# Layer 1's projection on raw rows: the mean in the matrix, 1/std in the eviction, results loaded three groups ahead

## The chip, the cores and the metric

The kernel runs on one core of a Trainium2 chip. The metric is device time in microseconds (us) of one execution; lower is better. Engines in this text: PE is TensorE (PEld its weight loads), DVE is VectorE, ACT is ScalarE, POOL is GpSimd, SP is SyncE, whose queue issues most transfers.

## The reference, cut to what matters

Two layers, each a graph attention and then a feed-forward part, on x of 3327 rows by 256. The part that the change touches is the entry of layer 1's attention:

```python
def _layernorm(x, axis=-1, eps=1e-5):
    m = jnp.mean(x, axis=axis, keepdims=True)
    v = jnp.var(x, axis=axis, keepdims=True)
    return (x - m) / jnp.sqrt(v + eps)

def _L1_gnn_ref(h, adj, W, a):
    wh = h @ W
    wh1 = wh @ a[:F_OUT, :]
    wh2 = wh @ a[F_OUT:, :]
    e = wh1 + wh2.T
    e = jnp.where(e > 0, e, ALPHA * e)
    e = jnp.where(adj > 0, e, NEG_BIG)
    attention = jax.nn.softmax(e, axis=-1)
    h_prime = attention @ wh
    return jax.nn.elu(h_prime)

x = x + _L0_gnn_ref(_layernorm(x), adj, ...)
x = x + _L0_ffn_ref(_layernorm(x)[None], ...)[0]      # 16 experts, the best 2 of each row
x = x + _L1_gnn_ref(_layernorm(x), adj, L1_gnn_W, L1_gnn_a)
x = x + _L1_ffn_ref(_layernorm(x)[None], ...)[0]      # 30 recurrent steps
```

So wh is the product of the normalized rows with W; the two score columns wh1 and wh2 are computed here as two more columns of the same product, from W a, so that the matrix has 258 columns.

## The kernel before, in words

x lies in SBUF as 26 tiles of 128 rows by 256. The stages follow each other: layer 0's projection, its attention, the experts (61 tiles of 128 listed rows, about 397 to 746 us), layer 1's projection (752 to 811 us), layer 1's attention, and 30 recurrent steps (on PE from about 1113 us).

**The experts.** `work_off` (L784) runs one tile of rows at a time: two products with w1 and w2 (L773), silu and multiply (L801, L805), the product with w3 (L812), a scaling (L815), and a scatter of the rows to `given` in DRAM (L816). On the way, at tile 16, it loads layer 1's parameters (`layer1_parameters`, L322: the matrix gW into `wv1`, the vectors ga, and `ones_r`, a tile of ones), and at tile 22 `score_vectors` (L334) computes the two score columns of `wv1`.

**Layer 1's projection.** `groups1` (L45) cuts the 26 tiles into seven groups: group 0 has two tiles, groups 1 to 6 have four. For each group:

- `add_results` (L885) loads the two results of every row from `given` (L891, two transfers on SP's queue into the buffers `th` and `z`, which have two copies each), adds them (L892, on POOL; for group 0 on DVE), and adds the sum to x (L894, DVE). Groups 0 and 1 are asked for ahead of the loop, group g + 2 while group g is worked on.
- `normalized` (L108) takes mean and variance on DVE (L114, L115), variance plus epsilon (`ve`, L117), its power -1/2 on POOL (`rstd`, L119), minus mean times rstd on POOL (`low`, L122, L123), and writes the normalized rows `xn` on ACT (L125, scale and bias of each row).
- `turned` (L133) transposes two tiles of `xn` on PE (L139, four instructions into a PSUM bank) and copies them to `hT` on ACT (L140).
- `products` (L149) multiplies each of the two tiles with `wv1` (L153, two matmuls of 258 columns a tile, each of them two records in the trace), one pair of tiles behind the transposes.
- `split1` (L904) evicts a product: 256 columns to `wh` on ACT (L905), the two scores to `sc.s` on DVE (L906). At a group's end `Scores.finish` (L180) makes exponentials on ACT (L181 to L183, full, part and row) and `minus` on DVE (L184).

The products go to six PSUM places (three names, two copies), the transposes to two. After the stage, `attend` (L188) transposes the row factors (L208, copied in L212), makes edges on ACT (L239), masks them on DVE (L244) and multiplies on PE (L249).

**What sets the order.** Each engine has one queue of instructions, in which it works in order. The tile framework's scheduler places the instructions of the stages into these queues; so on DVE the statistics of one group stand between the additions and the scores of others, and on POOL the order of the additions and of `rstd` and `low` is fixed: rstd, low and low of group 0, additions 1 and 2, rstd, low and low of group 1, addition 3, and so on. `project` and `normalized` serve layer 0 too, where normalized rows are written on DVE (L128).

Of the kernel before, what the change touches and what calls it, by code (L numbers as in the profile page):

```python
# [3 lines left out]

# [6 lines left out]
F32 = mybir.dt.float32  # L11
# [3 lines left out]
AF = mybir.ActivationFunctionType  # L15
ALU = mybir.AluOpType
# [3 lines left out]
P = 128  # L20
# [4 lines left out]
G = 4  # L25
MOST = 6
# [3 lines left out]
def gat_moe_gat_recurrent_ffn(ctx: ExitStack, tc: tile.TileContext, a: dict, out: bass.AP):  # L30
    nc = tc.nc
    N, D = a["x"].shape
    KD = D // P
# [9 lines left out]
    groups = [range(t, min(t + G, NT)) for t in range(0, NT, G)]  # L43
# [23 lines left out]
    x = state.tile([P, NT, D], F32, name="x")  # L67
# [37 lines left out]
    )  # L105
    nc.vector.tensor_scalar(real, real, 0.0, None, op0=ALU.is_gt)

    def normalized(src, dst, scale=1.0, by_act=False):  # L108

        n = len(src)  # L110
        mv = small.tile([P, MOST, 2], F32, name="mv")
        for j in range(n):
            st = small.tile([P, 6], F32, name="st")
            nc.vector.bn_stats(st, src[j])  # L114
            nc.vector.bn_aggr(mv[:, j, :], st)  # L115
        ve = small.tile([P, MOST], F32, name="ve")
        nc.vector.tensor_scalar(ve[:, :n], mv[:, :n, 1], EPS, 1.0 / scale**2, op0=ALU.add, op1=ALU.mult)  # L117
        r = small.tile([P, MOST], F32, name="rstd")
        power = nc.gpsimd.tensor_tensor(r[:, :n], ve[:, :n], neg_half[:, :n], ALU.pow)  # L119
        if by_act:  # L120
            low = small.tile([P, MOST], F32, name="low")
            nc.gpsimd.tensor_tensor(low[:, :n], mv[:, :n, 0], r[:, :n], ALU.mult)  # L122
            nc.gpsimd.tensor_scalar(low[:, :n], low[:, :n], -1.0, None, op0=ALU.mult)  # L123
            for j in range(n):
                nc.scalar.activation(dst[j], src[j], AF.Identity, scale=r[:, j : j + 1], bias=low[:, j : j + 1])  # L125
            return power.ins
        for j in range(n):
            nc.vector.tensor_scalar(  # L128
                dst[j], src[j], mv[:, j, 0:1], r[:, j : j + 1], op0=ALU.subtract, op1=ALU.mult
            )  # L130
        return power.ins

    def turned(two, work, ps):  # L133

        pt = ps.tile([P, 2, KD, P], F32, name="bank")
        hT = work.tile([P, 2, KD, P], F32, name="hT")
        for j in range(2):
            for k in range(KD):
                nc.tensor.transpose(pt[:, j, k, :], two[:, j, k * P : (k + 1) * P], ident)  # L139
        nc.scalar.copy(hT, pt)  # L140
        return hT

    def project(groups, wv, n_out, finish, work, ps, ps_p, by_act, aside):

        pending = None

        def products(hT, t):  # L149
            for j in range(2):  # L150
                p = ps_p()
                for k in range(KD):
                    nc.tensor.matmul(  # L153
                        p[:, :n_out], lhsT=hT[:, j, k, :], rhs=wv[:, k, :], start=(k == 0), stop=(k == KD - 1)
                    )
                finish(t + j, p)

        for ts in groups:
            n = len(ts)
            xn = work.tile([P, G, D], F32, name="xn")  # L160
            power = normalized([x[:, t, :] for t in ts], [xn[:, j, :] for j in range(n)], 1.0, by_act)
            aside(ts, power)
            for j0 in range(0, n, 2):
                hT = turned(xn[:, j0 : j0 + 2, :], work, ps)
                if pending:
                    products(*pending)
                pending = hT, ts[j0]
        products(*pending)

    class Scores:  # L170
# [9 lines left out]
        def finish(self, t0, t1):  # L180
            nc.scalar.activation(self.full[:, t0:t1], self.s[:, t0:t1, 1], AF.Exp)  # L181
            nc.scalar.activation(self.part[:, t0:t1], self.s[:, t0:t1, 1], AF.Exp, scale=ALPHA)
            nc.scalar.activation(self.row[:, t0:t1], self.s[:, t0:t1, 0], AF.Exp, scale=1.0 - ALPHA)  # L183
            nc.vector.tensor_scalar(self.minus[:, t0:t1], self.part[:, t0:t1], -1.0, None, op0=ALU.mult)  # L184
# [149 lines left out]
    def score_vectors():  # L334

        for k in range(KD):
            for s in range(2):
                tc.keep_in_program_order(
                    nc.vector.scalar_tensor_tensor(
                        prod, wv1[:, k, :D], 1.0, va[:, s, :], op0=ALU.mult, op1=ALU.mult,  # L340
                        accum_out=wv1[:, k, D + s : D + s + 1],
                    )
                )

    with ExitStack() as moe:
# [25 lines left out]
        def bank():  # L371
            return ps.tile([P, 512], F32, name="bank")

        with ExitStack() as pre:
# [63 lines left out]
                if ts is groups[3]:  # L438
                    take_graph(groups0[0], behind)

            project(groups, wv, D + 2 * H, split0, work, ps, bank, False, first_rows)
            nc.vector.tensor_scalar(wh[:, NT - 1], wh[:, NT - 1], real[:, 0:1], None, op0=ALU.mult)
            for ts in groups0[1:3]:
                behind = take_graph(ts, behind)
# [339 lines left out]
        def work_off(s0, s1, aside):  # L784

            hT = features_first(ahead.popleft())
            made = None
            for s in range(s0, s1 + 1):
                if s == FIRST:
                    for _ in aside:  # L790
                        pass
                    layer1_parameters()
                if s == FIRST + 6:
                    score_vectors()
                hidT = made
                if s < s1:
                    if s + 4 < s1:
                        ahead.append(gathered(s + 4))
                    pa = product(hT, ew[s % SETS][0])
                    act = edge("e")  # L800
                    nc.scalar.activation(act, pa, AF.Silu)  # L801
                    next(aside, None)
                    pb = product(hT, ew[s % SETS][1])
                    made = edge("pT")
                    nc.vector.tensor_tensor(made, act, pb, ALU.mult)  # L805
                    if s + 1 < s1:
                        hT = features_first(ahead.popleft())
                if s > s0:
                    w3 = ew[(s - 1) % SETS][2]
                    po = ps_o.tile([P, 512], F32, name="acc1")[:, :D]  # L810
                    for f in range(FH):
                        nc.tensor.matmul(po, lhsT=hidT[:, f, :], rhs=w3[:, f, :], start=(f == 0), stop=(f == FH - 1))  # L812
                    y0 = 6 * KD * HID + s % 2 * D
                    y = sets[1][:, y0 : y0 + D]
                    nc.vector.tensor_scalar(y, po, weight[:, s - 1 : s], None, op0=ALU.mult)  # L815
                    put = nc.gpsimd.indirect_dma_start(  # L816
                        out=given, out_offset=bass.IndirectOffsetOnAxis(ap=to[:, s - 1 : s], axis=0), in_=y,
                        in_offset=None,
                    )
                    tc.declare_no_dep(put.ins, group="given", reason="no two results have the same row")  # L820
                    tc.add_to_no_dep_group("given", put.ins)
                if s + SETS - 1 < s1:
                    weights(s + SETS - 1)
                next(aside, None)
# [52 lines left out]
    with ExitStack() as st:  # L877
# [4 lines left out]
        work = st.enter_context(tc.tile_pool(name="work2", bufs=2))  # L882
        ps = st.enter_context(tc.tile_pool(name="ps2", bufs=2, space=PSUM))
        ps_o = st.enter_context(tc.tile_pool(name="ps2o", bufs=2, space=PSUM))
        def add_results(some):  # L885
            for ts in some:
                n, two = len(ts), []
                for k, name in enumerate(("th", "z")):
                    here = slice(k * NP + ts[0] * P, k * NP + (ts[-1] + 1) * P)
                    two.append(steps.tile([P, G, D], F32, name=name)[:, :n, :])  # L890
                    nc.sync.dma_start(two[k], given[here, :].rearrange("(t p) d -> p t d", p=P))  # L891
                (nc.vector if ts is groups1[0] else nc.gpsimd).tensor_tensor(two[0], two[0], two[1], ALU.add)  # L892
                here = x[:, ts[0] : ts[-1] + 1, :]
                nc.vector.tensor_tensor(here, here, two[0], ALU.add)  # L894

        add_results(groups1[:2])
        count = 0

        def spot():
# [1 line left out]
            count += 1  # L901
            return ps_o.tile([P, 512], F32, name=f"acc{count % 3}")

        def split1(t, p):  # L904
            nc.scalar.copy(wh[:, t, 0, :D], p[:, :D])  # L905
            nc.vector.tensor_copy(sc.s[:, t, :, 0], p[:, D : D + 2])  # L906
            for ts in groups1:
                if t == ts[-1]:
                    sc.finish(ts[0], t + 1)

        project(
            groups1, wv1, D + 2, split1, work, ps, spot, True,
            lambda ts, power: add_results(groups1[groups1.index(ts) + 2 :][:1]),
        )
        nc.vector.tensor_scalar(wh[:, NT - 1], wh[:, NT - 1], real[:, 0:1], None, op0=ALU.mult)

# [144 lines left out]
```

## Time and profile before

| what | us |
|---|---|
| runs: median (lowest to highest of 3) | 2020.62 (2019.47 to 2022.0) |
| the profiled execution | 2019.73 |
| its span | 2017.6 |
| PE, DVE, ACT, POOL busy over the span | 1937.5, 1300.5, 1106.0, 955.3 |
| last scatter of the experts issued | 746.39 |
| first result transfer of layer 1 issued | 752.52 |
| first transpose of layer 1's projection | 760.97 |
| last product of the projection ends | 808.1 |
| first product of layer 1's attention | 811.25 |

The profile is of one execution. In its tables an entry such as "x4" counts instructions; a timeline line has the start in us from the span's start, the busy time, the engine, the line of the code, the operation with output<-inputs, and in brackets how long the engine idled before and what ended the idling. A line of the waits has the waiting instruction, the one waited for, and the sum, the number and the longest of these waits in us. PEclk is the share of its full clock that PE was granted.

### The profile page before, as it was taken

The numbers are of one execution on the slowest core, as the hardware profiler recorded it, in microseconds if no ns is written. First come the engines' busy times: TensorE is split into PE (matmuls) and PEld (weight loads), VectorE is DVE, ScalarE is ACT, GpSimd is POOL, SyncE is SP. The second block draws the span as 40 slices with busy tenths as digits, with TensorE's granted clock in tenths as the row PEclk, the third lists the DMA queues.
The fourth block names the chain that finished last, engine by engine and source line by source line (L and its number), as shares of the span: only waits on it lengthen the run. The fifth ranks groups of instructions, "written<-read, shape, count | busy, mean of one in ns | idle before, by whom it ended". The sixth has DMA issues, their size and how long they took to land.

```text
span 2017.6 us, 33598 instructions
## 1 busy us (share of the span) xinstructions
PE 1937.5 (96%) x12028; PEld 1752.4 (87%) x12028; DVE 1300.5 (64%) x3845; ACT 1106.0 (55%) x1445; POOL 955.3 (47%) x884
## 2 busy tenths in 40 slices
PE   7999999999999977999999999999999999999998
PEld 6999999999999975888888888888888888888887
DVE  6887888732222215567676777777777777777777
ACT  2976766621111116666555665665666666666664
POOL 3020212453333315001000677877877887777785
PEclk9999999999999997999999999999999999999999
DMA  8978141199999853000000000000000000000003
GB/s 163 118 99 118 9 76 49 42 314 332 349 331 306 293 168 120 9 9 16 9 9 16 27 1 1 1 1 1 1 1 1 1 1 1 1 1 1 1 1 115
DMA packets 139754, 157.08 MB, mean 78 GB/s; under 512 B 52027, under 2 KB 99364, under 8 KB 139586
## 3 DMA queue, kind: packets, MB, share of 16 engines
q1 hardware_dynamic: 123466, 122.05, 19.8%
q0 software_dynamic: 11440, 28.09, 8.1%
q10 hardware_dynamic: 4680, 4.76, 0.7%
q8 instruction: 98, 1.61, 0.3%
q14 instruction: 70, 0.57, 0.1%
HBM read 164.58 MB, written 29.78 MB: 96 GB/s over the span
## 4 chain that ended last, share of the span: by engine, by line
PE 67%; issue 10%; POOL 5%; ACT 5%; DVE 4%; DMA 4%; SPq 0%; POOLq 0%; DVEq 0%; ACTq 0%
PE po L996 35%; PE acc L249 23%; PE pt L990 5%; ACT zT L992 5%; POOL given L816 2%; DVE pT L244 2%; POOL rb L717 2%; DMA given<-wh,to 2%; DMA wh<-in_w_dram 1%; DMA lists<-pair,ati 1%; PE acc L153 1%; PE bank L139 1%; PE bank L486 1%; POOL rstd L119 1%; PE bank L208 0%
## 5 line engine op out<-in xcount | busy, mean ns | idle before, releaser
L996 PE MATMUL po<-wc,zT 128*128 128x256 f32 x3120 | 706.1, 383 | 21.7 <-ACT zT L992 21.1
L996 PEld LDWEIGHTS po<-wc,zT 128*128 128x128 f32 x3120 | 583.5, 190 | 124.6 <-ACT zT L992 50.0
L249 PE MATMUL acc<-wh,pT 128*128 128x129 f32 (+1 forms) x4056 | 606.5, 311 | 2.0 <-DVE pT L244 1.8
L249 PEld LDWEIGHTS acc<-wh,pT 128*128 128x128 f32 x4056 | 561.7, 191 | 40.1 <-DVE pT L244 3.7
L239 ACT ACTIVATE e<-rb,minus,full 128x384 f32<-128x384 f32 (+3 forms) x494 | 400.4, 824 | 180.0 <-DVE pT L244 164.0
L982 POOL TENSOR_TENSOR th<-th,x 128x1024 f32<-128x1024 f32 (+1 forms) x210 | 459.9, 2206 | 64.0 <-ACT th L980 64.0
L244 DVE SCALAR_TENSOR_TENSOR pT<-e,part,adjT 128x384 f32<-128x384 f32 (+3 forms) x494 | 380.7, 774 | 138.4 <-PE acc L249 118.8
L1001 DVE SCALAR_TENSOR_TENSOR x<-po,rr,bb 128x256 f32<-128x256 f32 x780 | 324.8, 477 | 119.1 <-PE po L996 114.2
L992 ACT COPY zT<-pt 128x1024 f32<-128x1024 f32 (+1 forms) x210 | 199.1, 948 | 333.8 <-PE pt L990 333.8
L988 DVE BATCH_NORM_STATS2 stats<-z 128x6 f32<-128x256 f32 x780 | 283.6, 415 | 117.2 <-ACT z L983 117.2
L119 POOL TENSOR_TENSOR rstd<-ve,neg_half 128x4 f32<-128x4 f32 (+3 forms) x28 | 31.1, 1110 | 413.2 <-DVE ve L117 317.5
L971 POOL TENSOR_TENSOR rr<-rr,neg_half 128x4 f32<-128x4 f32 (+1 forms) x210 | 207.5, 988 | 17.4
L983 ACT ACTIVATE z<-th 128x1024 f32<-128x1024 f32 (+1 forms) x210 | 210.6, 1003 | 0.4 <-POOL th L982 0.3
L980 ACT ACTIVATE th<-x 128x1024 f32<-128x1024 f32 (+1 forms) x210 | 199.3, 995 | 2.2 <-DVE x L128 1.3
L990 PE MATMUL pt<-ident,z 128*128 128x128 f32 x1560 | 190.9, 273 | 2.5 <-DVE high L926 2.5
L990 PEld LDWEIGHTS pt<-ident,z 128*128 128x128 f32 x1560 | 178.6, 141 | 14.8 <-issue 2.9
L773 PEld LDWEIGHTS bank<-hT,wh 128*128 128x128 f32 x1280 | 149.2, 192 | 6.0 <-issue 1.7
L773 PE MATMUL bank<-hT,wh 128*128 128x128 f32 x1280 | 150.5, 275 | 3.2 <-DMA wh<-in_w_dram 3.2
L805 DVE TENSOR_TENSOR pT<-e,bank 128x512 f32<-128x512 f32 x61 | 41.9, 687 | 167.2 <-PE bank L773 167.1
L801 ACT ACTIVATE e<-bank 128x512 f32<-128x512 f32 x61 | 36.4, 597 | 195.2 <-PE bank L773 186.8
L816 POOL DMA_INDIRECT given<-wh,to x61 | 60.2, 987 | 165.7 <-DVE wh L815 148.4
L552 POOL DMA_INDIRECT lists<-pair,ati x52 | 61.1, 1176 | 133.9 <-DVE ati L539 43.5
(183 smaller groups left out, 1261.3 us busy)
## 6 DMA issues: line engine op xcount, KB each, us to landing
wh<-in_w_dram SPq DMA_DIRECT2D x120, 512.0 KB
first_set<-in_w_dram SPq DMA_DIRECT2D x63, 512.0 KB
in_bytes<-in_adj_dram POOLq DMA_DIRECT2D x3, 2496.0 KB, 28.3
x<-in_x_dram SPq DMA_DIRECT2D x6, 512.0 KB
th<-given SPq DMA_DIRECT2D x6, 512.0 KB
z<-given SPq DMA_DIRECT2D x6, 512.0 KB
kept<-x SPq DMA_DIRECT2D x8, 384.0 KB
old<-kept SPq DMA_DIRECT2D x6, 512.0 KB
```

The source lines that it names most:

```text
L239: nc.scalar.activation(e[:, : n * P], rb[:, : n * P], AF.Relu, scale=sc.full[:, j, h : h + 1], bias=sc.minus[:, j, h : h + 1],)
L244: masked = nc.vector.scalar_tensor_tensor(pT[:, : n * P], e[:, : n * P], sc.part[:, j, h : h + 1], adjT[:, j // 2, ts[0] * P : (ts[-1] + 1 ...
L249: nc.tensor.matmul(po[c], lhsT=pT[:, c * P : (c + 1) * P], rhs=wh[:, j, h, :], start=(j == 0 and c % per_bank == 0), stop=(j == NT - 1), s ...
L773: nc.tensor.matmul(p[:, f, :], lhsT=w[:, k, f * P : (f + 1) * P], rhs=hT[:, k, :], start=(k == 0), stop=(k == KD - 1),)
L971: nc.gpsimd.tensor_tensor(r[:, :n], r[:, :n], neg_half[:, :n], ALU.pow)
L982: nc.gpsimd.tensor_tensor(th[:, :n, :], th[:, :n, :], hs, ALU.add)
L983: nc.scalar.activation(z[:, :n, :], th[:, :n, :], AF.Silu, scale=1.0 / S)
L988: nc.vector.bn_stats(stats[:, j, :], z[:, j, :])
L990: nc.tensor.transpose(pt[:, j, k, :], z[:, j, k * P : (k + 1) * P], ident)
L992: nc.scalar.copy(zT[:, :n, :, :], pt[:, :n, :, :])
L996: nc.tensor.matmul(po[:, j, :], lhsT=zT[:, j, k, :], rhs=wc[:, k, :], start=(k == 0), stop=(k == KD - 1),)
L1001: nc.vector.scalar_tensor_tensor(x[:, ts[0] + j, :], po[:, j, :], rr[:, j : j + 1], bb, op0=ALU.mult, op1=ALU.add)
```

## The change

In layer 1 the rows are no longer normalized ahead of the product. The rows x go to the transposes as they are. The mean is taken out by the matrix: `without_mean`, called once at tile 26 of the experts, subtracts from every column of `wv1` that column's mean over its 256 entries, through a product with ones on PE and a combined multiply and add on DVE for each half. The factor 1/std of a row is applied when the product is evicted: a scale in ACT's copy and a multiply in DVE's copy of the scores. `low` and `xn` fall away in layer 1; statistics and `rstd` stay. The result buffers rotate over three names with two copies each, and group g + 3 is asked for while group g is worked on. Layer 0 computes as before.

```diff
-    def normalized(src, dst, scale=1.0, by_act=False):
+    def inverse(src, scale=1.0):
...
         power = nc.gpsimd.tensor_tensor(r[:, :n], ve[:, :n], neg_half[:, :n], ALU.pow)
-        if by_act:
-            low = small.tile([P, MOST], F32, name="low")
-            nc.gpsimd.tensor_tensor(low[:, :n], mv[:, :n, 0], r[:, :n], ALU.mult)
-            nc.gpsimd.tensor_scalar(low[:, :n], low[:, :n], -1.0, None, op0=ALU.mult)
-            for j in range(n):
-                nc.scalar.activation(dst[j], src[j], AF.Identity, scale=r[:, j : j + 1], bias=low[:, j : j + 1])
-            return power.ins
...
+        return r, mv, power.ins
...
+    def without_mean(wv, n_out, ones, p):
+
+        for k in range(KD):
+            nc.tensor.matmul(p[:, :n_out], lhsT=ones, rhs=wv[:, k, :], start=(k == 0), stop=(k == KD - 1))
+        for k in range(KD):
+            nc.vector.scalar_tensor_tensor(
+                wv[:, k, :], p[:, :n_out], -1.0 / D, wv[:, k, :], op0=ALU.mult, op1=ALU.add
+            )
...
-                finish(t + j, p)
+                finish(t + j, p, *([r[:, j : j + 1]] if raw else []))
...
-            xn = work.tile([P, G, D], F32, name="xn")
-            power = normalized([x[:, t, :] for t in ts], [xn[:, j, :] for j in range(n)], 1.0, by_act)
+            tiles = [x[:, t, :] for t in ts]
+            if raw:
+                r, _, power = inverse(tiles)
+            else:
+                xn = work.tile([P, G, D], F32, name="xn")
+                power = normalized(tiles, [xn[:, j, :] for j in range(n)])
             aside(ts, power)
             for j0 in range(0, n, 2):
-                hT = turned(xn[:, j0 : j0 + 2, :], work, ps)
+                hT = turned(x[:, ts[j0] : ts[j0] + 2, :] if raw else xn[:, j0 : j0 + 2, :], work, ps)
...
+                if s == FIRST + 10:
+                    without_mean(wv1, D + 2, ones_r, bank())
...
+        names = cycle(("th", "z", "zT"))
...
-                for k, name in enumerate(("th", "z")):
+                for k in range(2):
                     here = slice(k * NP + ts[0] * P, k * NP + (ts[-1] + 1) * P)
-                    two.append(steps.tile([P, G, D], F32, name=name)[:, :n, :])
+                    two.append(steps.tile([P, G, D], F32, name=next(names))[:, :n, :])
...
-        add_results(groups1[:2])
+        add_results(groups1[:3])
...
-        def split1(t, p):
-            nc.scalar.copy(wh[:, t, 0, :D], p[:, :D])
-            nc.vector.tensor_copy(sc.s[:, t, :, 0], p[:, D : D + 2])
+        def split1(t, p, r):
+            nc.scalar.activation(wh[:, t, 0, :D], p[:, :D], AF.Copy, scale=r)
+            nc.vector.tensor_scalar(sc.s[:, t, :, 0], p[:, D : D + 2], r, None, op0=ALU.mult)
...
-            lambda ts, power: add_results(groups1[groups1.index(ts) + 2 :][:1]),
+            lambda ts, power: add_results(groups1[groups1.index(ts) + 3 :][:1]),
```

More of the change, by code (lines that the diff above doesn't have):

```diff
@@ L3 @@
 from functools import partial
+from itertools import cycle
 import concourse.bass as bass
@@ L119, in normalized @@
         power = nc.gpsimd.tensor_tensor(r[:, :n], ve[:, :n], neg_half[:, :n], ALU.pow)
-        if by_act:
-            low = small.tile([P, MOST], F32, name="low")
-            nc.gpsimd.tensor_tensor(low[:, :n], mv[:, :n, 0], r[:, :n], ALU.mult)
-            nc.gpsimd.tensor_scalar(low[:, :n], low[:, :n], -1.0, None, op0=ALU.mult)
-            for j in range(n):
-                nc.scalar.activation(dst[j], src[j], AF.Identity, scale=r[:, j : j + 1], bias=low[:, j : j + 1])
-            return power.ins
-        for j in range(n):
+        return r, mv, power.ins
+    def normalized(src, dst, scale=1.0):
+        r, mv, power = inverse(src, scale)
+        for j in range(len(src)):
             nc.vector.tensor_scalar(
@@ L130, in normalized @@
             )
-        return power.ins
+        return power
+    def without_mean(wv, n_out, ones, p):
[5 more added lines that the diff above has]
+            )
     def turned(two, work, ps):
@@ L141, in turned, with project, products @@
         return hT
-    def project(groups, wv, n_out, finish, work, ps, ps_p, by_act, aside):
+    def project(groups, wv, n_out, finish, work, ps, ps_p, aside, raw=True):
         pending = None
-        def products(hT, t):
+        def products(hT, t, r):
             for j in range(2):
@@ L155, in products @@
                     )
-                finish(t + j, p)
+                finish(t + j, p, *([r[:, j : j + 1]] if raw else []))
         for ts in groups:
             n = len(ts)
-            xn = work.tile([P, G, D], F32, name="xn")
-            power = normalized([x[:, t, :] for t in ts], [xn[:, j, :] for j in range(n)], 1.0, by_act)
+            tiles = [x[:, t, :] for t in ts]
[4 more added lines that the diff above has]
+                power = normalized(tiles, [xn[:, j, :] for j in range(n)])
             aside(ts, power)
             for j0 in range(0, n, 2):
-                hT = turned(xn[:, j0 : j0 + 2, :], work, ps)
+                hT = turned(x[:, ts[j0] : ts[j0] + 2, :] if raw else xn[:, j0 : j0 + 2, :], work, ps)
                 if pending:
                     products(*pending)
-                pending = hT, ts[j0]
+                pending = hT, ts[j0], r[:, j0 : j0 + 2] if raw else None
         products(*pending)
@@ L439, in first_rows @@
                     take_graph(groups0[0], behind)
-            project(groups, wv, D + 2 * H, split0, work, ps, bank, False, first_rows)
+            project(groups, wv, D + 2 * H, split0, work, ps, bank, first_rows, False)
             nc.vector.tensor_scalar(wh[:, NT - 1], wh[:, NT - 1], real[:, 0:1], None, op0=ALU.mult)
@@ L911, in gat_moe_gat_recurrent_ffn @@
         project(
-            groups1, wv1, D + 2, split1, work, ps, spot, True,
-            lambda ts, power: add_results(groups1[groups1.index(ts) + 2 :][:1]),
+            groups1, wv1, D + 2, split1, work, ps, spot,
+            lambda ts, power: add_results(groups1[groups1.index(ts) + 3 :][:1]),
         )
```

## The prediction

> **What bounds the kernel now.** I read the page's chain first. Layer 1's projection is a short stage between the experts and the attention, so I then read busy time by stretch, the waits of 752 to 812 us, and the timeline.
>
> Busy time and granted clock (PEclk) by stretch, projection only:
>
> ```profile
> core 0: us, PE busy (x) PEld busy (x) DVE busy (x) ACT busy (x) POOL busy (x), PEclk, DMA share, GB/s
> 752.00:760.30 8.30, 0.00 (x0) 0.00 (x0) 2.60 (x8) 0.00 (x0) 1.16 (x3) 0.50 0.76 231
> 760.30:770.00 9.70, 4.61 (x13) 3.05 (x13) 6.78 (x21) 2.72 (x6) 8.74 (x6) 0.68 0.73 236
> 770.00:780.00 10.00, 9.76 (x37) 7.46 (x38) 9.30 (x25) 8.81 (x23) 6.92 (x6) 0.70 0.72 214
> 780.00:790.00 10.00, 6.34 (x32) 4.48 (x31) 5.01 (x20) 5.27 (x16) 6.51 (x7) 0.98 0.16 51
> 790.00:800.00 10.00, 9.24 (x37) 7.72 (x38) 2.94 (x18) 7.70 (x23) 2.92 (x6) 0.68 0.00 0
> 800.00:810.40 10.40, 10.25 (x60) 8.90 (x60) 2.20 (x13) 8.28 (x28) 0.00 (x0) 1.00 0.01 2
> ```
>
> No engine is full throughout. PE pauses, loses its clock twice, and is full only after 790. Who it waited for:
>
> ```profile
> PEld bank L139 <- ACT xn L125: 26.7, 11, 15.8
> ACT xn L125 <- POOL low L123: 25.2, 4, 19.3
> POOL rstd L119 <- DVE ve L117: 16.5, 4, 11.6
> DVE s L906 <- ACT wh L905: 12.1, 14, 1.7
> DVE x L894 <- POOL th L892: 9.3, 3, 4.3
> ```
>
> PE's transposes wait for ACT's normalized rows, these for `low` on POOL, that for DVE's statistics and for POOL's additions. Single steps in the timeline:
>
> ```profile
> 760.73 2.35 POOL L892 TENSOR_TENSOR th<-th,z 128x1024 f32<-128x1024 f32 x1 [0.45 <-issue]
> 763.11 1.23 DVE L894 TENSOR_TENSOR x<-x,th 128x1024 f32<-128x1024 f32 x1 [4.32 <-POOL th L892]
> 763.34 3.21 POOL L892 TENSOR_TENSOR th<-th,z 128x1024 f32<-128x1024 f32 x1 [0.26 <-DMA z<-given]
> ...
> 786.05 2.34 POOL L892 TENSOR_TENSOR th<-th,z 128x1024 f32<-128x1024 f32 x1
> ...
> 790.76 0.69 PE L139 MATMUL bank<-ident,xn 128*128 128x128 f32 x2 [3.11 <-ACT xn L125]
> ...
> 804.44 3.65 PE L153 MATMUL acc<-wv,hT 128*128 128x258 f32 x16
> ...
> 811.25 6.99 PE L249 MATMUL acc<-wh,pT 128*128 128x257 f32 x31
> ```
>
> The last addition starts at 786.05, PE is fed without a break only from 790.76, its last product ends at 808.1, the attention starts at 811.25. From there PE bounds; nothing changes.
>
> **What the Trainium skill says.** "SBUF — State Buffer", Who interferes with whom: a VectorE instruction with two SBUF inputs and a GpSimd one that reads SBUF exclude each other. The trace agrees: POOL's addition of 763.34 took 3.21 instead of 2.35 us while DVE's ran to 764.34. "TensorE: Matmul & The Clock Gate", Part 1: half rate until about 3.4 us were busy. Agrees in kind: eight product records took 3.42 us at 762.88 and 1.91 at 783.56; after 769.99 some 7 busy us passed before full rate. "ScalarE: Activation LUTs", What ACT_TABLE_LOAD costs: 186 ns + 0.833 ns per element, plus 93 per pointer operand. Agrees: L125, two pointers, 597 ns measured against 585.
>
> **The change, part by part.**
>
> *Mean out of the matrix* (at tile 26 of the experts). Two matmuls of 258 columns, 0.22 us each warm (L153: 1.75 us for eight). One expert tile takes 5.52 us (L801 to L801: 734.87, 740.39) and PE is full in it, so +0.44 on the path; 0 if hidden. The same edit's two DVE operations (0.48 each, as L815) stand ahead of a multiply for which DVE idles 3.16 us: free; without that cover 1 us.
>
> *Removed*: 26 ACT normalizations (L125: four in 2.08 us, 13.5 in sum) and 7 pairs of `low` on POOL (0.20 and 0.23 with gaps, about 0.6 a group, 4 in sum). They cost the path only what stands in the waits above; the walk below says how much. *Evictions with a scale*: 26 times 0.373 us (L905) becomes, with one pointer, 0.49 by the skill's formula; bounds 0.373 and 0.60 (L125). ACT then needs 2 x 0.40 + 0.59 + 0.15 = 1.5 us per pair of tiles (at the upper bound 1.9), PE 2.19 (0.44 transposes, 1.75 products): hidden. The score scaling costs 0.16 like the copy (L906); at worst as L184's 0.17.
>
> *Moved wait*: transposes wait only for the added rows; 1/std is awaited by the evictions. Behind a waiting eviction stand ACT's next hT copy, hence PE's next product, and on DVE the score scalings with additions and `ve` behind them. I walked the queues in the changed kernel's built order, in the profile's time, with POOL's addition at 2.35 us (760.73), DVE's at 1.23 (763.11), `ve` at 0.17 (L117), rstd at 1.04 (L119), hT copies at 0.59 (L140), and the exclusion of the two adders; that order puts POOL's rstd of group 1 behind addition 2, of group 4 behind addition 6, and DVE's `ve` of a group behind the next group's addition and one or two score scalings:
>
> - Group 0: rows added 757.6, as before; product cold to 762.9.
> - Group 1: POOL adds 760.0 to 762.35 (0.7 earlier: no `low` ahead), DVE to 763.6.
> - Group 2: the data land about 763.3 as before, DMA being busy anyway; POOL to 766.0, DVE to 767.2. Only then `ve` (0.2) and rstd (1.04) of group 1: 768.5.
> - Group 3: POOL 768.6 to 770.95, DVE 772.2; aggregate, score, `ve` to 772.8; rstd of group 2 773.9.
> - Group 4: POOL 774.0, DVE 777.6; rstd of group 3 779.4.
> - Group 5: POOL 779.5, DVE 783.1. Group 6: POOL 783.1 to 785.45, DVE 786.7; rstd of group 4 stands behind it on POOL: 786.6.
> - PE: cold for group 1's transposes from 763.65 and its first product, to 768.9; warm from about 770 (some 6 us of unbroken work; before it took 7; each pair that stays cold longer costs 2.1). Then 2.19 us a pair: the last product of group 3 and the first of group 4 end at 780.6 and 782.8, with waits of a few tenths for rows. Group 4's evictions wait to 786.6, the hT copy of group 5 behind them ends at 788.55: PE loses about 2.8 us. Three more pairs, paced by ACT, and the last: 796.5.
>
> Then eviction, row copy, exponentials, edge, mask: 2.7 us (3.14 before; one of two row copies now stands behind the first edges, 0.45). Attention starts at 799.2 instead of 811.25: 12.05 less; with 0.44 of the matrix **11.6 us**. *Three groups ahead*: data arrive at 3.64 us a group (1.05 MB at 288 GB/s, the mean of the DMA view's busy slices), POOL's additions come every 4.6, so it is worth about 0; up to 1 for the last two additions, which follow each other. SP issues the same 14 transfers and nothing else then; no queue is passed.
>
> The profiled execution lasted 2019.73 us: span 2017.6 and 2.1 around it, 0.9 below the median of the runs, 2020.62. So 2008.1 against itself, **2009.0** as a median.
>
> **Rivals.**
> *PE full from group 1*: the eviction wait and POOL's order cost nothing. From 768.9, 11 products and 10 quadruples of transposes, 23.7 us: 792.6, attention at 795.3. Gain 15.95 - 0.44 = 15.5: 2005. For: PE has work queued from 776. Against: rstd of group 4 stands behind two additions on POOL.
> *Adders stay at the old pace*: POOL's additions ran 760.73 to 786.05, 5.06 us each; if the sum of addition, DVE addition, `ve`, rstd (4.8) grows by the scores ahead of `ve`, addition 6 stays at 785 to 786 and evictions wait for later groups too: end 799 to 802, gain 6 to 9: 2013.
> *The removed work was hidden*: PE would be held elsewhere, gain under 4. Against: 50 us of listed waits on xn, on PE and its weight loads.
> *Slower: the clock stays at half*. With gaps each group PE might never get its full rate. A cold pair takes 8 x 0.43 + 4 x 0.22 = 4.3 us, 2.1 more than warm; 12 pairs from 763.65 end at 815.5, attention at 818.2, 7 us late: 2028. It decides from 15.6/2.1, more than 7 of the 10 later pairs cold. Against: cold, PE is busy 8.6 us a group against 4.6 of the adders, so it has no gaps and the clock comes.
>
> **How the numbers follow.** Forecast (gain 10 to 13.5) 0.55; PE full (2004.5 to 2007) 0.15; old pace (gain 4 to 10) 0.22; hidden 0.05; slower 0.03. Range 2004.5 to 2014.5, leaving out the last two and the weak end of the old pace. A difference of 0.2% (4 us) is about what can be told from none: faster 0.92, same 0.05, slower 0.03.
>
> **What would show it.** Right: transposes of group 1 start at the end of DVE's addition; L139 no longer waits on ACT; PE's longest late pause lies before group 5's products, behind an eviction waiting on rstd; the last POOL addition about 783; last product 796.5; expert stage half a microsecond longer. Wrong: low PEclk after 775, evictions above 0.6 us, transfers as the releaser of POOL's additions after 766, or additions over 5 us apart.

## The result, and the profile after

The changed kernel takes 2010.47 us (median of 6 runs, 2009.49 to 2013.27), the kernel before 2021.99 (6 runs beside them). The ratio is 0.9945, 95% interval 0.9933 to 0.9958: 11.1 us less, between 8.5 and 13.5. Forecast were 2009.0 us and 11.6 us less.

The profiled execution of the changed kernel lasted 2013.27 us (span 2011.6), only 6.0 us of span less than before. It is the slowest of its six runs, and the trace shows a likely reason: during the experts PE stood still for 3.62 us (until 443.98, waiting for a row copy on ACT, which had itself waited for something that the profile calls only "remote"). The change does nothing there. Over the fourteen profiles of this study the projection begins (its first memset on DVE) anywhere from 750.6 to 761.8 us, so the experts vary by more than most edits below are worth. I therefore measure the *stage*: from that memset to the first product of layer 1's attention. Before, this is 752.91 to 811.25, **58.3 us**; changed, 756.72 to 804.75, **48.0 us**. From there to the end it is 1206.4 us before and 1206.9 after: no change.

Busy time and granted clock by stretch of the changed kernel's projection (columns as in the prediction's table: PE, PEld, DVE, ACT and POOL busy with their instruction counts, then PEclk, the share of time that DMA was busy, and GB/s):

```profile
755.70:764.10 8.40, 1.91 (x6) 1.44 (x7) 2.60 (x8) 0.58 (x1) 0.72 (x1) 0.50 0.78 236
764.10:773.80 9.70, 8.21 (x28) 6.20 (x28) 5.81 (x20) 4.32 (x10) 7.28 (x4) 0.56 0.96 290
773.80:783.80 10.00, 10.00 (x56) 8.69 (x55) 7.18 (x29) 6.13 (x18) 6.47 (x5) 1.00 0.63 204
783.80:793.80 10.00, 7.54 (x31) 5.60 (x29) 7.98 (x24) 3.92 (x13) 5.37 (x4) 0.83 0.01 2
793.80:803.80 10.00, 9.97 (x58) 8.85 (x58) 4.11 (x23) 7.66 (x24) 1.95 (x2) 1.00 0.01 2
```

PE is now full from 773.8 and has its full clock there; before, it was full at its full clock only in the last stretch. One hole is left, between 783.8 and 793.8. The waits of the stage, in full lines of the same kind as before:

```profile
PE bank L147 <- DVE x L911: 12.7, 2, 11.2
ACT wh L922 <- POOL rstd L120: 6.9, 3, 5.9
PE bank L147 <- DVE minus L197: 2.5, 1, 2.5
ACT wh L922 <- DMA z<-given: 2.2, 1, 2.2
PE acc L162 <- ACT hT L148: 0.7, 1, 0.7
```

The transposes (L147 here) no longer wait for ACT; most of the 12.7 us is the wait for group 0's data ahead of the first one. ACT's evictions (L922) have taken over the wait for rstd, once for 5.9 us. And PE's late hole of 2.5 us is put down to DVE's `minus`, whose result the transposes don't read. The timeline shows what came before it on DVE:

```profile
767.37 3.36 POOL L909 TENSOR_TENSOR z<-z,zT 128x1024 f32<-128x1024 f32 x1
...
785.74 2.35 POOL L909 TENSOR_TENSOR th<-th,z 128x1024 f32<-128x1024 f32 x1
785.82 3.36 DVE L911 TENSOR_TENSOR x<-x,z 128x1024 f32<-128x1024 f32 x1 [2.22 <-POOL z L909]
...
789.33 0.69 PE L147 MATMUL bank<-ident,x 128*128 128x128 f32 x4 [2.46 <-DVE minus L197]
...
789.81 3.57 PE L162 MATMUL acc<-wv,hT 128*128 128x258 f32 x8
...
791.89 0.47 ACT L922 ACTIVATE wh<-acc,rstd 128x256 f32<-128x256 f32 x1 [5.87 <-POOL rstd L120]
...
804.75 1.57 PE L262 MATMUL acc<-wh,pT 128*128 128x257 f32 x6 [0.61 <-DVE pT L257]
```

POOL's addition of group 6 starts at 785.74, 0.08 us ahead of DVE's addition of group 5, and DVE's takes 3.36 instead of 1.23 us: it ends at 789.18, 1.1 us after POOL's (788.09), as if it had run only once POOL had finished. PE's transposes need these rows: PE pauses 2.46 us, and the eight product records after the pause (group 4's second pair of tiles) take 3.57 instead of 1.91 us.

### The profile page after: what moved, and what is told of

Read it like the earlier page. It is cut to its first block, busy times and chain, and to the rows that moved or that the text cites. A ratio compares the mean times of both kernels' runs of the same rounds, so it can differ in the third digit from the quotient of the medians.

```text
span 2011.6 us, 33554 instructions
## 1 busy us (share of the span) xinstructions
PE 1936.9 (96%) x12032; PEld 1754.0 (87%) x12032; DVE 1299.7 (65%) x3847; ACT 1096.0 (54%) x1419; POOL 951.3 (47%) x870
## 4 chain that ended last, share of the span: by engine, by line
PE 69%; issue 9%; POOL 5%; ACT 5%; DVE 4%; DMA 2%; another core or an unknown queue 0%; SPq 0%; POOLq 0%; DVEq 0%; ACTq 0%
PE po L1013 35%; PE acc L262 23%; PE pt L1007 5%; ACT zT L1009 5%; DVE pT L257 2%; POOL given L831 2%; POOL rb L730 2%; PE bank L786 2%; DMA given<-wh,to 2%; PE acc L827 1%; PE bank L499 1%; PE acc L162 1%; PE bank L221 1%; PE bank L147 0%
```

## The experiments

The theory: PE had been starved by a chain of waits, and the moved wait feeds it; what is left is set by the two adders, their order at the shared port, and rstd. The rivals: the removed work (`low` on POOL) is what counts; the loads are. Each run was compared with the kernel before on the same chip; "stage" is from its profile.

| run | stage, us | ratio to before (95%) |
|---|---|---|
| changed kernel | 48.0 | 0.9945 (0.9933 to 0.9958) |
| changed kernel again | 48.0 | 0.9955 (0.9941 to 0.9968) |
| loads alone | 57.2 | 0.9996 (0.9986 to 1.0006) |
| 1/std ahead of the transposes | 54.0 | 0.9974 (0.9965 to 0.9983) |
| mean out eight times | 48.2 | 0.9997 (0.9988 to 1.0006) |
| two groups ahead, twice | 52.6, 51.0 | 0.9955 (0.9936 to 0.9974), 0.9958 (0.9944 to 0.9971) |
| group 6 on DVE | 48.4 | 0.9950 (0.9930 to 0.9970) |
| and additions one group ahead, twice | 44.8, 46.5 | 0.9949 (0.9931 to 0.9967), 0.9933 (0.9920 to 0.9946) |
| and minus on ACT | 45.0 | 0.9940 (0.9927 to 0.9953) |
| additions one ahead, group 6 on DVE, loads two ahead, twice | 44.2, 45.8 | 0.9937 (0.9924 to 0.9951), 0.9952 (0.9937 to 0.9966) |

**Which part brings the gain.** First the moved wait is undone, which also brings ACT's 26 multiplications back:

```diff
+                xn = work.tile([P, G, D], F32, name="xn")
+                for j in range(n):
+                    nc.scalar.activation(xn[:, j, :], x[:, ts[j], :], AF.Copy, scale=r[:, j : j + 1])
...
-            nc.scalar.activation(wh[:, t, 0, :D], p[:, :D], AF.Copy, scale=r)
+            nc.scalar.copy(wh[:, t, 0, :D], p[:, :D])
```

> The changed kernel, but ACT multiplies the rows by 1/std before the transposes, and evictions are plain copies: the mean stays in the matrix, low stays away, only the moved wait is undone. My theory, the moved wait is the larger part of the gain: stage 54 to 57 us (58.3 before, 48.0 changed), transposes again waiting for ACT. Rival, removing low from POOL is what gives the gain: stage 48 to 50 us.

The stage is 54.0 us, inside the theory's span and far from the rival's. Its waits are those of the kernel before:

```profile
ACT xn L174 <- POOL rstd L120: 28.2, 4, 18.5
PEld bank L147 <- ACT xn L174: 23.4, 6, 14.8
PE bank L147 <- ACT xn L174: 20.9, 4, 14.4
```

So of the 10.3 us of the stage, 6.0 come from moving the wait behind the product, and 4.3 from what goes without it (`low` and the loads ahead). The totals agree less sharply: 0.9974 against the changed kernel's 0.9945 and 0.9955 makes 3.8 to 5.9 us, measured on different chips. No run takes away `low` alone, so the 4.3 us stay unsplit. Then the loads alone, in the kernel before:

```diff
+        names = cycle(("th", "z", "zT"))
...
-                for k, name in enumerate(("th", "z")):
+                for k in range(2):
...
-        add_results(groups1[:2])
+        add_results(groups1[:3])
...
-            lambda ts, power: add_results(groups1[groups1.index(ts) + 2 :][:1]),
+            lambda ts, power: add_results(groups1[groups1.index(ts) + 3 :][:1]),
```

> The kernel before with the loads three groups ahead in three rotating names and nothing else. My theory: the loads alone carry nothing, since POOL's additions there wait for low and for DVE, not for data: stage 57 to 59.5 us (58.3 before). Rival, the loads carry 4 us of the gain, as the run with two groups ahead (52.6 against 48.0) could be read: 53 to 55 us.

57.2 us and a ratio of 0.9996: in the old order the third group brings next to nothing. In the new order the opposite edit was tried, twice:

```diff
-        names = cycle(("th", "z", "zT"))
+        names = cycle(("th", "z"))
...
-        add_results(groups1[:3])
+        add_results(groups1[:2])
...
-            lambda ts, power: add_results(groups1[groups1.index(ts) + 3 :][:1]),
+            lambda ts, power: add_results(groups1[groups1.index(ts) + 2 :][:1]),
```

> The changed kernel with results asked for two groups ahead in two buffer names again. Measure: the stage's length, from its first memset to the attention's first product; 58.3 us before, 48.0 in the changed kernel. My theory: the loads carry nothing, POOL's and DVE's additions set the pace; 47.5 to 48.5 us. It can be lower by up to 4 if group 6's data come so late that DVE's addition of group 5 gets the SBUF port ahead of POOL's addition of group 6. Rival, the third group is needed to keep additions fed: 50 us or more, and transfers end POOL's waits.

> The changed kernel with loads two groups ahead once more, for a second profile. In the first, POOL's addition of group 2 took the port 0.04 us ahead of DVE's addition of group 1 (3.35 us), and the stage lasted 52.6 us. My theory, the loads carry nothing and that order is chance, as it fell the other way in the run with group 6 on DVE and two groups ahead (stage 44.2 us): if DVE is first here, 48 to 50.5 us, if POOL is first, 51.5 to 53. Rival, two groups ahead cost 4 us in themselves: 52 us or more with DVE first too.

Here the theory missed: 52.6 us, not 48, and 51.0 the second time, just under the 51.5 to 53 given for POOL first. The rival's "50 us or more" was met, but not its sign: transfers ended 2.5 us of POOL's waits in each run, DVE's instructions some 24. The timeline of the first of these runs (POOL's two additions are one line of 4.63 us):

```profile
764.32 4.63 POOL L909 TENSOR_TENSOR th<-th,z 128x1024 f32<-128x1024 f32 x2 [1.68 <-DMA th<-given]
```

```profile
766.69 3.35 DVE L911 TENSOR_TENSOR x<-x,th 128x1024 f32<-128x1024 f32 x1 [4.92 <-POOL th L909]
```

POOL goes from its addition of group 1 to that of group 2 without a gap, and DVE's addition of group 1 is blocked for 2.1 us; with three groups ahead POOL's second addition started 0.08 us after DVE's (767.37 and 767.29) and it was POOL that waited. The first transposes of group 1 start 14.2 and 14.3 us after the memset instead of 11.9: that is 2.3 and 2.4 of the 4.6 and 3.0 us. POOL waits 0.8 and 0.7 us for group 6's data, but PE's lag behind the changed kernel doesn't grow there: it is 2.8 and 3.0 us at group 4's first products and 2.9 and 3.0 at group 5's. In the first run, slow-clock records after that (2.91 us for group 5's first eight) explain most of the rest. POOL was first both times, which speaks against the chance that I had expected. What sets it for each kernel stays open; the two instructions become ready within 0.1 us of each other. The totals don't show this loss: 3.0 to 4.6 us would be 0.0015 to 0.0023, and 0.9955 and 0.9958 lie beside the changed kernel's 0.9945 and 0.9955, within each other's intervals. That data as such are not needed earlier is shown below, with the two-groups version of the better order.

**The price of the mean.** In the changed kernel's timeline the pass stands between two third products of the experts:

```profile
552.88 1.89 PE L827 MATMUL acc<-first_set,pT 128*128 128x256 f32 x8
554.61 1.03 PE L135 MATMUL bank<-wv,ones_r 128*128 128x258 f32 x4
555.49 3.73 PE L786 MATMUL bank<-hT,wh 128*128 128x128 f32 x32
559.05 0.38 PE L777 MATMUL acc<-ident,rb 128*128 128x128 f32 x2
559.27 1.89 PE L827 MATMUL acc<-wh,pT 128*128 128x256 f32 x8
```

Four records, not two, and 6.39 us from third product to third product instead of 5.52: 0.87 us. To see whether it is on the path, it was done eight times over (a matrix whose columns have mean zero stays as it is):

```diff
-                    without_mean(wv1, D + 2, ones_r, bank())
+                    for _ in range(8):
+                        without_mean(wv1, D + 2, ones_r, bank())
```

> The changed kernel, taking the mean out of the matrix eight times instead of once at tile 26 (columns of mean zero stay as they are). In the profile one pass showed four PE records, so my theory now is 0.87 us for a pass, on the path: the distance between the third products of tiles 25 and 26 grows from 5.52 to about 12.5 us if only PE counts, up to 16 if each pass also waits for DVE's two operations of the pass before. As the prediction sized it, 0.44 a pass: 9 us. Rival, hidden beside the weights' transfers: 5.5 us.

The scheduler spread the passes over two tiles. From the third product at 545.78 to the second one after it, at 567.21, it takes 21.43 us instead of 11.04: 10.4 for eight passes. Of these 7.0 are PE's own, and the timeline lists 1.9 of the rest as waits for DVE between passes. The whole run is 0.0042 of 2018.7, or 8.5 us, slower than the changed kernel on the same chip, near the 9.5 us that the profile gives for the seven added passes. So a pass is on the path, and the single one costs 0.87 us by the profile.

**What holds the changed kernel now.** The hole before group 5 looks like the blocked addition. But rstd of group 4 ended only at 791.86, and evictions waited for it. Group 6's results were therefore added on DVE, which leaves POOL nothing to block with:

```diff
-                (nc.vector if ts is groups1[0] else nc.gpsimd).tensor_tensor(two[0], two[0], two[1], ALU.add)
+                (nc.vector if ts in (groups1[0], groups1[-1]) else nc.gpsimd).tensor_tensor(two[0], two[0], two[1], ALU.add)
```

> The changed kernel with group 6's two results added on DVE, so that POOL can't hold the port against DVE's addition of group 5, which took 3.36 instead of 1.23 us. In the built order DVE's ve of group 4 stands behind both additions of group 6. My theory, two waits ended nearly together, the blocked addition and the eviction waiting for rstd of group 4, and the second takes the place of the first: stage 47 to 48.5 us against 48.0. Rival, the blocked addition alone made PE pause and lose its clock: stage 43.5 to 45 us.

48.4 us, as the theory had it. In its timeline the addition of group 5 has its own length again, and the next wait is there:

```profile
789.85 1.23 DVE L911 TENSOR_TENSOR x<-x,z 128x1024 f32<-128x1024 f32 x1 [2.23 <-POOL z L909]
...
792.05 1.21 DVE L909 TENSOR_TENSOR th<-th,z 128x1024 f32<-128x1024 f32 x1
793.37 1.21 DVE L911 TENSOR_TENSOR x<-x,th 128x1024 f32<-128x1024 f32 x1
794.50 0.16 DVE L118 TENSOR_SCALAR ve<-mv 128x4 f32<-128x4 f32 x1
794.81 1.02 POOL L120 TENSOR_TENSOR rstd<-ve,neg_half 128x4 f32<-128x4 f32 x1 [4.99 <-DVE s L923]
795.86 0.47 ACT L922 ACTIVATE wh<-acc,rstd 128x256 f32<-128x256 f32 x1 [5.82 <-POOL rstd L120]
...
797.50 2.01 PE L162 MATMUL acc<-wv,hT 128*128 128x258 f32 x8 [3.47 <-ACT hT L148]
```

`ve` of group 4 stands behind both additions of group 6 on DVE, rstd behind `ve`, the evictions behind rstd, the hT copy behind the evictions, and PE waits 3.47 us for it. In the changed kernel `ve` of group 4 stood behind the blocked addition of group 5 instead. Two waits ended close together; removing one showed the other. Both should go if the additions are asked for later, so that `ve` of group 4 stands ahead of group 6's:

```diff
-        add_results(groups1[:3])
+        load_results(groups1[:3])
+        add_results(groups1[:1])
...
+        def ahead_of(ts, power):
+            g = groups1.index(ts)
+            load_results(groups1[g + 3 :][:1])
+            add_results(groups1[g + 1 :][:1])
```

(`load_results` and `add_results` are the two halves of the old `add_results`; group 6 stays on DVE.)

> As the run with group 6 on DVE, and the additions are asked for one group ahead instead of three, the loads still three: then ve of group 4 stands ahead of both additions of group 6 in DVE's queue. My theory, with both waits gone PE runs on warm from about 772 us to the end: stage 44 to 45.5 us, total 2.5 to 4 us below the changed kernel. Rival, the additions' pace is the bound: 47 to 49 us.

> The changed kernel once more, unaltered, for a second profile of it and for a ratio on the same chip as the next run. My theory: POOL's addition of group 6 takes the port ahead of DVE's addition of group 5 again (it was ready 0.08 us earlier), so the stage lasts 47.5 to 48.7 us and DVE's addition of group 5 over 3 us. Rival, that order is chance: 44 to 46 us this time, the addition 1.2 us.

> The version with additions one group ahead and group 6's on DVE once more, for a ratio on the same chip as the changed kernel. My theory: stage 44 to 46 us again, total 2 to 4 us below the changed kernel, ratio to the kernel before 0.992 to 0.9935 against 0.9945. Rival, the 44.8 us were an early warm clock (group 1's transposes ran at full rate in that profile, not in the changed kernel's): 46.5 to 48 us.

The changed kernel repeated itself: 48.0 us, DVE's addition of group 5 again 3.35 us. One thing differs, and it bares the second wait:

```profile
785.17 0.63 PE L147 MATMUL bank<-ident,x 128*128 128x128 f32 x4 [2.44 <-DVE minus L197]
785.64 1.91 PE L162 MATMUL acc<-wv,hT 128*128 128x258 f32 x8
...
789.70 2.01 PE L162 MATMUL acc<-wv,hT 128*128 128x258 f32 x8 [1.72 <-ACT hT L148]
```

Here PE kept its full clock after the pause, so the eight records took 1.91 us, and PE then waited 1.72 us for the hT copy behind the evictions. In the first profile slow records filled that time. Group 5's products start 37.1 us after the memset in both: the eviction wait sets them, not the slow records.

The better order gave 44.8 us, then 46.5, at the lower edge of the rival's span; of the eviction wait 0.81 us is left in both. Its first ratio, 0.9949, shows none of the 2.5 to 4 us expected over the changed kernel, which did not run on that chip; on the second chip its ratio was 0.9933, the changed kernel's 0.9955. In the second profile group 1's data came 0.7 us later after the memset, and DVE held something small for long:

```profile
769.18 2.35 POOL L916 TENSOR_TENSOR th<-th,z 128x1024 f32<-128x1024 f32 x1
769.19 2.37 DVE L197 TENSOR_SCALAR minus<-part 128x2 f32<-128x2 f32 x1
```

A negation of two elements a row, 0.17 us elsewhere, lasted as long as POOL's addition under it. It was moved to ACT (in both layers' attentions):

```diff
-            nc.vector.tensor_scalar(self.minus[:, t0:t1], self.part[:, t0:t1], -1.0, None, op0=ALU.mult)
+            nc.scalar.activation(self.minus[:, t0:t1], self.part[:, t0:t1], AF.Copy, scale=-1.0)
```

> The version with additions one group ahead and group 6's on DVE, and the negation minus computed on ACT in both attentions. In the two profiles of that version DVE's negation of a few elements took 2.2 to 2.4 us once or twice, each time under one of POOL's additions, and the stage 44.8 and 46.5 us. My theory, that wait for the port delays the next addition: stage 43.5 to 45.2 us, no DVE instruction of the stage but additions above 0.5 us. Rival, the two profiles differ by the arrival of group 1's data (0.7 us) and the phase of the clock: 44.8 to 46.5 us again.

45.0 us, and no DVE instruction of the projection but the additions above 0.5 us. The time lies in both spans. The block is gone; its price shows only if the stage is split, at the start of group 1's second pair of products (here in the first and second profile of the better order and in this one):

```profile
775.63 1.91 PE L162 MATMUL acc<-wv,hT 128*128 128x258 f32 x8
769.81 1.91 PE L162 MATMUL acc<-wv,hT 128*128 128x258 f32 x8
768.42 1.91 PE L162 MATMUL acc<-wv,hT 128*128 128x258 f32 x8
```

Up to there the three took 16.1, 17.6 and 17.2 us from their memsets (759.57, 752.21, 751.23), from there to the attention 28.7, 28.9 and 27.9. So 44.8 and 46.5 differ by what came before, data and the clock of group 1's records, and hardly by the blocked negation; moving it to ACT took 0.9 to 1.0 us off the second part, in one profile. The changed kernel's two profiles take 17.1 us up to this point and 31.0 and 30.9 after it, so the better order gains 2.0 to 2.2 us there.

Last, the better order with only two groups loaded ahead (`cycle(("th", "z"))`, and 2 for 3 in the loads):

> The version with additions one group ahead and group 6's on DVE (stage 44.8 and 46.5 us), with loads only two groups ahead in two names. My theory, what two groups ahead cost in the changed kernel was the order at the port (POOL's addition of group 2 was ready 0.04 us before DVE's of group 1, which took 3.35 us) and 0.8 us of waiting for group 6's data: here the first stays and the second is hidden, stage 46.5 to 48.7 us. Rival, the data themselves come late: 49 us or more, with transfers ending POOL's waits after group 2.

> The version with additions one group ahead, group 6's on DVE and loads two groups ahead once more. Its first profile had the shortest stage, 44.2 us. My theory: with DVE first at the port 44 to 46 us, with POOL first at group 2 about 2.1 more; total 3 to 5 us below the changed kernel's ratio of 0.9945 to 0.9955, so 0.992 to 0.994. Rival, the third group in flight is needed: 48 us or more.

44.2 and 45.8 us (28.8 and 28.3 of them in the second part): below my first span, within the second, and no worse than three groups ahead. DVE was first at the port in both (its addition of group 1 took 1.23 us). So the third group in flight is not what PE needs. The second run's ratio, 0.9952, fell short of the 0.992 to 0.994 that I gave it. Of all versions, the five profiles of this order have the shortest stages (44.2 to 46.5), 1.5 to 3.9 us below the changed kernel, and ratios of 0.9933 to 0.9952; only where both ran on one chip (0.9933 and 0.9955) is the total's gain over the changed kernel visible, and there the intervals still overlap a little.

## Why the prediction was right

The direction, the size and the main mechanism held: 11.1 us measured, 11.6 forecast, and 6.0 of the stage's 10.3 us are the moved wait. By its steps:

- *Mean out of the matrix, +0.44 us on the path.* On the path, yes; the size was wrong by two. I divided 1.75 us for eight L153 records by eight and called the quotient a matmul; a matmul of this type leaves two records (104 for the projection's 52). Measured 0.87.
- *Eviction with one pointer, 0.49 us.* Measured 0.47 (L922), 0.02 below what the Trainium skill's formula in "ScalarE: Activation LUTs", What ACT_TABLE_LOAD costs, gives; hidden beside PE but for the wait for rstd, as said.
- *The walk of the queues.* Shifted by 3.81 us (the two memsets), POOL's additions of groups 3 to 6 were forecast for 772.4, 777.8, 783.3 and 786.9 and came at 773.22, 778.26, 783.43 and 785.74. The full clock was forecast from about 773.8; from 773.78, with group 1's second pair, the products run at full rate. The end of group 4's first products, 786.6, came at 786.87.
- *The late pause.* This is the step that failed. I let DVE's addition of group 5 end before POOL's of group 6 began, at 783.1, and put PE's pause, 2.8 us, behind group 4's evictions, with POOL's order holding rstd. POOL was first, by 0.08 us, and DVE's addition took 3.36 us. That made a pause for the rows of group 5 that I hadn't forecast (2.46 us). It also held `ve` of group 4, which stands behind it on DVE: rstd ended at 791.86 instead of 790.4 (shifted), the hT copy of group 5 at 793.80 instead of 792.4. The wait that I had named was there (5.87 us on ACT) and set the start of group 5's products; in the profiled run slow records (1.7 us more) filled it, in the repeat it shows as 1.72 us. So PE lost 4.2 us in this place, not 2.8. The evidence for the exclusion was in my own first fence; what I didn't do was to ask for each pair of adders which one is ready first.
- *Length of the stage.* Last product forecast at 796.5, 800.3 with the shift; measured 801.97, and 1.4 of these 1.7 us are the late hT copy. Then 2.78 us to the attention, forecast 2.7. So 10.3 us instead of 12.05; with the 0.87 the profile accounts for 9.4 us, inside the measured interval of 8.5 to 13.5. The total can't tell 9.4 from 11.6, so that 11.1 came out so near is in part luck.
- *Three groups ahead, 0 to 1 us.* In the old order 1.1 us of stage and no measurable total, in the better order nothing; but within the changed kernel's own order two groups cost 3.0 to 4.6 of stage, which I did not foresee: 2.3 and 2.4 of it because the order at the port turned. No total shows it.
- *Rivals.* PE full from group 1 (stage 42.4) was not reached by any version; that the removed work was hidden (gain under 4) is out, with 8.5 us as the least of the interval; the clock at half throughout did not occur (its break-even uses 15.6 us where my sums give 15.5); the additions kept a pace of 4.2 us (764.92 to 785.74, five steps), not the old 5.06.

## What to carry to other kernels

Where the statistics of a row come late, as here, a per-row factor that commutes with a matmul can go behind it: the product then waits for the data alone, and the statistics have until the eviction. When two engines exclude each other at a port, work out for each pair which instruction is ready first; here the loser waited until the winner was done, 2.1 us on DVE behind a POOL addition of 2.35, and so did all that stood behind it in its queue. And when a wait goes, look for the one that ended just before it, as the group 6 edit shows: the time stays until both are gone.

## What the runs showed of the hardware

- A DVE operation on two elements a row took 2.37 us under one of POOL's additions, and 0.17 us elsewhere. The kernel before has it too: there `ve`, four elements a row, ended with POOL's addition at 771.6:

```profile
769.27 2.34 POOL L892 TENSOR_TENSOR th<-th,z 128x1024 f32<-128x1024 f32 x1
769.63 2.02 DVE L117 TENSOR_SCALAR ve<-mv 128x4 f32<-128x4 f32 x1
```

  The exclusion that "SBUF — State Buffer", Who interferes with whom, in the Trainium skill describes, and for which it names tensor_scalar under conditions that no run here tests, fits these times: the two-element operation was held up 2.2 us, as long as a large one (2.1 us for the addition of group 5).
- The clock after a pause is not a matter of the pause's length alone: in two runs of one and the same kernel eight records took 3.57 us after a pause of 2.46 us, and 1.91 after one of 2.44. After 3.47 us in the run with group 6 on DVE they took 2.01.
